# Four residual graph layers on one core: a list schedule with one port for VectorE's two-operand and GpSimd's operations, layer 2's second aggregates placed later, and a buffer of its own for group 1's adjacency

## The chip, the cores and the metric

The kernel runs on one core of a Trainium2 chip. The metric is the device time of one execution in microseconds (us). The kernel before takes 2507.59 us, the median of three runs (2506.04 to 2507.76). Its trace was taken in one profiled execution of 2507.6 us.

## The reference

There are 128 graphs of 128 nodes with 512 features each, and one adjacency of 128x128 per graph. Four layers follow each other. Each adds its result to x and normalises every row of the sum. All is float32.

```python
deg = adj.sum(-1)
d   = (deg + 1) ** -0.5
L   = d[:, :, None] * (adj + I) * d[:, None, :]
# layer 0
x = layernorm(x + relu((L @ x) @ W0 + b0))
# layer 1
q, k = split(x @ Wqk.T, 2);  v = x @ Wv.T          # 64 features each in q and k
w = softmax(((q @ k.T) / 8 * adj).sum(-1), over nodes)
x = layernorm(x + w[:, :, None] * v)
# layer 2
agg = (adj @ x) / max(deg, 1e-6)
x = layernorm(x + relu(concat([x, agg]) @ W2.T))
# layer 3
x = layernorm(x + L @ (x @ W3 + b3))
```

The kernel computes layer 0 and layer 3 as (L @ x) @ W, and layer 3's bias as the row sums of L times b3.

## The kernel before

**Tiles and stages.** The 128 graphs are worked on in 32 groups of G = 4. A group's x is one tile of 128 nodes by 4 graphs by 512 features, and it stays in place through all four layers. The four graphs form two pairs q; in each pair, r = 0 or 1 names the graph. "The first half" below is r = 0, graphs 0 and 2; "the second half" is r = 1, graphs 1 and 3.

A product of a group with a 512x512 weight (`project`, line 511 and below) is taken by blocks of 256 with seven block products in the place of eight, in Winograd's form. Their names are B11, T1, B21, B22, T2, T3 and T4. Four of them need sums of blocks of the left operand (`left_sums`, tiles s1 to s4) and of the weight (`weight_sums`, made once). The left operand has the features on the partitions. It is either an aggregate (`aggregate`, line 452 and below: TensorE multiplies x by a transposed adjacency, and ScalarE copies the result out of the tile p_agg), or a transpose of x, named xT1 for layer 1 and xT2 for layer 2. In the loop x is transposed through DRAM and by VectorE (`turn_x`), at the start and the end by TensorE (`turn_on_tensor`). Layer 2 has two left operands, xT2 and agg2, so each of its products has twice the matmuls.

The results of the products are combined on VectorE in the blocks u5, u2, sa and sb, which are added to x. In the profile they carry an o, for layers 0, 2 and 3, or a v, for layer 1 (u_o, s_v, x<-u_v). A half of x is then normalised by `norm_stats`: VectorE makes the statistics (bnv, mvo), GpSimd the reciprocal root, ScalarE applies them. Layer 3 is normalised by `norm_last`, on ScalarE. PSUM is held in five buffers "pb", for the products (p_o, p_v), and three "pt", for aggregates, transposes and small products. The matmuls are float32, and each shows as two records in the profile. One block product of a group in layers 0, 1 and 3 has 16 records, one of layer 2 has 32; an aggregate of one graph has 8.

`hooks` of a `project` name work that TensorE does right after one of its products; `tails` holds the last product of a `project` until `finish_tails` issues it.

**The order of the work.** `begin` handles groups 0 and 1 through their first layers (lines 814 to 837). After it, each turn t of the loop (lines 840 to 861) interleaves four groups' stages: layer 0 of group t, the load and preparation of group t+1, layer 2 of group t-1, the aggregates of layer 0 of group t+1, layer 1 of group t, layer 3 of group t-1, and at the end the transposes and aggregates of layer 2 of group t. What is left of the last group follows on lines 863 to 870, pair by pair.

**The planner.** Nothing is issued while this code runs. Class `Plan` records every operation with what it reads and writes (`record`, `touch`), and `schedule` (lines 194 to 255) then orders each engine's queue as a list schedule. TensorE's operations keep the order in which the code states them. Every other operation has a due time, worked back from the TensorE operation that needs it (lines 207 to 216). `estimate` (line 284) gives each a duration. The loop at lines 225 to 254 then takes, engine by engine, the operation with the earliest due time among those whose operands are ready. `emit` issues all of them from line 263, so that every row of the profile shows L263; rows are told apart by engine, operation and tile. Each engine works through its own queue in order, so an operation that waits holds everything behind it.

**Preparation of a group.** `load(t)` issues adj and x on SP (the DMA queue's own engine). The tag "adj" has one buffer, so adj of t+1 can only land when VectorE has used that of t. `prep_rows` makes on VectorE deg (row sums of adj), dh, dm, rdeg and the two matrices in `ana`, with the power d on GpSimd. `prep_transpose` turns `ana` on TensorE (tile p_a, into anT and arT) for the first groups, and `prep_turn` does it through DRAM in the loop.

**Layer 1's weights.** `l1_scores` gives, on VectorE, scr, w and rs; TensorE transposes w (p_w); then mx, e and the division make a softmax, and TensorE turns it back (p_ws, ws). All of it stands between layer 1's first products.

Of the kernel before, what the change touches and what calls it, by code (L numbers as in the profile page):

```python
# [18 lines left out]
G = 4  # L19
# [99 lines left out]

class Op:  # L120
    def __init__(self, engine):
        self.engine, self.dur, self.lat, self.size, self.calls, self.preds, self.succs = engine, 0, 0, 0, [], set(), []
        self.last, self.start, self.end = float("inf"), None, None


class Plan:

# [27 lines left out]
    def record(self, engine, method, args, kw):  # L157
        op = self.group if self.group is not None and engine == "tensor" else Op(engine)
        op.calls.append((method, args, kw))
        dur, op.lat, op.size = self.est(engine, method, args, kw)  # L160
        op.dur += dur
        out = kw.get("out", args[0] if args else None)
        outs = [v for v in (out, kw.get("accum_out")) if isinstance(v, Ref)]
        ins = [v for k, v in list(enumerate(args)) + list(kw.items())
               if isinstance(v, Ref) and v is not out and k != "accum_out"]
        for v in ins:
            self.touch(op, v, False)
        for v in outs:
            self.touch(op, v, True)
        op.preds.discard(op)  # L170
        if op is not self.group:
            self.ops.append(op)
# [21 lines left out]
    def schedule(self):  # L194
# [21 lines left out]
            op.last = min(op.last, due - op.dur)  # L216
        queue = {e: [] for e in self.ENGINES}
        waiting = {op: len(op.preds) for op in self.ops}
        free, bus = dict.fromkeys(self.ENGINES, 0), 0
        pe = [op for op in self.ops if op.engine == "tensor"]  # L220
        for op in self.ops:
            if not op.preds:
# [2 lines left out]
        while len(done) < len(self.ops):  # L225
            best = None
            for e in self.ENGINES:
                q = queue[e]
                if e == "tensor":
                    q = [c for c in q if c[2] is pe[0]]  # L230
                if not q:
                    continue
                at = max(free[e], min(c[0] for c in q))
                pick = min((c for c in q if c[0] <= at), key=lambda c: (c[2].last, c[1]))
                for c in q:
                    if at < c[0] < at + pick[2].dur and c[2].last < at + pick[2].dur and c[2].last < pick[2].last:
                        pick, at = c, c[0]
                if best is None or at < best[0]:
                    best = at, e, pick
            at, e, pick = best  # L240
            queue[e].remove(pick)
            op = pick[2]
            op.start, op.end = at, at + op.dur
            free[e] = op.end
            if e == "sync":
                bus = max(bus, op.end + self.LAND) + op.size / self.BUS
                op.lat = max(op.lat, bus - op.end)
            if e == "tensor":
                pe.pop(0)
            done.append(op)  # L250
            for s in op.succs:
                waiting[s] -= 1
                if not waiting[s]:
                    queue[s.engine].append((max(p.end + self.hop(p, s) for p in s.preds), number[s], s))
# [29 lines left out]
def estimate(engine, method, args, kw):  # L284

    out = args[0]
    n = out.idx.size if isinstance(out, Ref) else 0
    if engine == "tensor":
        return (max(109, 0.85 * n) if method == "transpose" else 2 * max(100, 0.833 * n + 2.5)), 100, 0
    if method == "dma_start":  # L290
        size = max(int(np.prod(v.shape)) if isinstance(v, bass.AP) else v.idx.size * 32 * len(v.quads) for v in args)
        return 470, Plan.LAND + size / 60, size
    if engine == "scalar":
        return (380 if method == "activation" else 160) + 0.83 * n, 0, 0
    if engine == "gpsimd":
        if ALU.pow in args:
            return 400 + 150 * n, 0, 0
        return 250 + 2.2 * n, 0, 0
    if method in ("bn_stats", "tensor_reduce"):
        n = args[1].idx.size  # L300
    both = [v for v in args[1:] if isinstance(v, Ref) and v.idx.size == n and v.tile.args[3]["tag"] not in ("pb", "pt")]
    return 160 + (1.3 if len(both) > 1 else 1.04) * n, 0, 0

@with_exitstack
def kernel(
# [30 lines left out]
    st = {}  # L338

    def load(t):  # L340
        a = ap.tile([P, G, P], FP, tag="adj", name=f"adj_{t}", bufs=1)
        nc.sync.dma_start(a, adj[t * G:(t + 1) * G].rearrange("g n m -> n g m"))
        xi = xp.tile([P, G, F], FP, tag="x", name=f"x_{t}")
        for g in range(0, G, 2 if t == 0 else G):
            k = slice(g, g + (2 if t == 0 else G))
            nc.sync.dma_start(xi[:, k], x[t * G:(t + 1) * G][k].rearrange("g n f -> n g f"))
        st["adj", t], st["x", t] = a, xi


    load(0)  # L350

    def weight(src, name, queue, turned=False):

# [153 lines left out]
    def finish_tails():  # L507
        while tails:
            tails.pop(0)()

    def project(name, t, parts, first, c11, fin, hooks=None, after=lambda: None, early=True,
# [7 lines left out]
        def region():  # L519
            return ps_b.tile([P, 2, H], FP, tag="pb", name=f"p_{name}_{t}")[:, qs]  # L520

        def product(p, k, fresh):
            with nc.unit():
                for q in pairs:
                    for i, (left_, w) in enumerate(parts):
                        for c in range(2):
                            nc.tensor.matmul(p[:, q - pairs[0], :], left_[k][:, q, c, :], w[:, k, c, :],
                                             start=(fresh and q == pairs[0] and i == 0 and c == 0),
                                             stop=(i == len(parts) - 1 and c == 1), skip_group_check=True)
            for f in hooks.get(k, ()):  # L530
                f()
# [105 lines left out]
    def l0_out(t, hooks=None, pairs=(0, 1)):  # L637
# [13 lines left out]
            nc.vector.tensor_tensor(c, p, bias(0), ALU.add)  # L651
            fin(0, 0, c)

        project("o0", t, [(st["agg0", t], w0_sb)], first, c11, fin, hooks, pairs=pairs)


    def l1_turn(t, turn=turn_x):
        left("xT1", t)
        for r in range(2):
            turn("xT1", t, r)  # L660
        st["x1T", t] = st["xT1", t]
        left_sums("xT1", t)

    def l1_qk(t, r):

# [59 lines left out]
    def l1_out(t, hooks=None):  # L725
# [14 lines left out]
        def weights():  # L740
            l1_weights(t)
            for f in pending:
# [1 line left out]

        pending = []
        hooks[T3] = [weights] + hooks[T3]
        project("v", t, [(st.pop(("xT1", t)), wv_sb)], copy_first, lambda p, b: fin(0, 0, p), fin, hooks,
                early=False, when=when)


# [3 lines left out]
            turn_x("xT2", t, r)  # L754
        left_sums("xT2", t)

    def l2_agg(t):
        left("agg2", t)
        for g in (0, 2, 1, 3):
            aggregate("agg2", t, g, st["arT", t])  # L760
        left_sums("agg2", t)

    def l2_both(t):

        left("xT2", t)
        left("agg2", t)
        for r in range(2):
            turn_on_tensor("xT2", t, r)
            for g in (r, 2 + r):
                aggregate("agg2", t, g, st["arT", t])  # L770
        left_sums("xT2", t, nc.vector)
        left_sums("agg2", t)

    def l2_out(t, hooks=None, pairs=(0, 1)):
        fin = relu_add(t, pairs)
        project("o2", t, [(st["xT2", t], w2x_sb), (st["agg2", t], w2a_sb)],
                copy_first, lambda p, b: fin(0, 0, p), fin, hooks, pairs=pairs)


# [18 lines left out]
    def l3_out(t, left="agg3", pairs=(0, 1)):  # L798
        def fin(r, h, blk):
            z = half(st["x", t], r, h, pairs)  # L800
            nc.vector.tensor_tensor(z, blk, z, ALU.add)

        project("o3", t, [(st[left, t], w3_sb)], copy_first, lambda p, b: fin(0, 0, p), fin,
                after=lambda: store(t), pairs=pairs)

    def store(t):
# [7 lines left out]
    def begin():  # L814

        prep_rows(0)
        load(1)
        prep_transpose(0)
        weight_sums(w0_sb, nc.gpsimd)
        l0_agg(0, nc.vector, ONE_BY_ONE)  # L820
        prep_rows(1)
        l0_out(0, {B21: [lambda: prep_transpose(1)], B22: [lambda: l0_agg(1)]})
        finish_tails()
        weight_sums(wv_sb, nc.vector)
        l0_out(1)
        l1_turn(0, turn_on_tensor)
        finish_tails()
        for r in range(2):
            l1_qk(0, r)
        for w in (w2x_sb, w2a_sb, w3_sb):  # L830
            weight_sums(w, nc.gpsimd)
        l1_turn(1)
# [1 line left out]
        finish_tails()  # L834
        for r in range(2):
            l1_qk(1, r)
        l2_both(0)

    begin()
    for t in range(1, NT):  # L840
        u = t - 1
        if t > 1:
            l0_out(t)
        if t < last:
            load(t + 1)
            prep_rows(t + 1)
            prep_turn(t + 1)
        if t > 1:
            tails.append(lambda: l1_turn(t))
        l2_out(u, {T3: [lambda: l1_qk(t, 0)]} if t > 1 else {})  # L850
        if t < last:
            l0_agg(t + 1)
        finish_tails()
# [4 lines left out]
        l3_out(u)  # L858
        if t < last:
            l2_turn(t)  # L860
            l2_agg(t)

    l2_both(last)
    for q in range(2):
        l2_out(last, pairs=(q,))
    for q in range(2):
        l3_agg_pair(last, q, nc.gpsimd)
        l3_bias(last, (2 * q, 2 * q + 1))
# [34 lines left out]
```

## Time and profile before

| | before |
|---|---|
| median of three runs | 2507.59 us |
| profiled execution | 2507.6 us |
| its span, first to last instruction | 2505.8 us |
| mean granted TensorE clock | 0.996 |
| TensorE matmul busy | 2466.6 us, 98% |
| VectorE busy | 1785.2 us, 71% |
| GpSimd busy | 1350.2 us, 54% |
| ScalarE busy | 973.2 us, 39% |
| HBM | 96 GB/s over the span |

PE is TensorE, PEld its weight loads, DVE VectorE, ACT ScalarE, POOL GpSimd, SP the engine that issues DMAs. A row such as `2.46 DVE L263 ... x<-s_v,ws,x ... x2` begins with the time from the span's start and the length, both in us, of a run of like instructions on one engine, and gives then the output, the inputs, the shapes and the number of instructions. `[0.19 <-DVE u_o]` says that the engine had been idle for 0.19 us and that VectorE's writing of u_o ended it. A row of a table of windows gives the stretch, its length, and then for TensorE, its weight loads, VectorE, ScalarE and GpSimd the busy time with the number of instructions; the granted clock, DMA's busy share and GB/s close it. A row of waits gives the waiting engine and tile, who ended the wait, the sum in us, the number of waits, and the longest.

### The profile page before, as it was taken

Reading aid. Unit: us, or ns where it says so; the run is one execution under the profiler, and the core shown is the slowest. Engines: PE = TensorE matmul, PEld = TensorE weight load, DVE = VectorE, ACT = ScalarE, POOL = GpSimd, SP = SyncE. Lnnn points to the kernel's source line nnn. Section 1 sums busy time; section 2 is a strip of 40 time slices with the busy share of each in tenths; the row PEclk is TensorE's granted clock in tenths of the full one; section 3 lists DMA queues with packets and bytes.
Section 4 is the critical chain, followed back from the end, with each engine's and each line's share of the span. In section 5 each row is a group of like instructions: output and inputs, shape, how many; then the busy total and the mean of one; then the engine's idle time right before and its main releaser. Section 6 shows DMA issues by size and latency. Waiting matters only on the chain.

```text
span 2505.8 us, 37042 instructions
## 1 busy us (share of the span) xinstructions
PE 2466.6 (98%) x13470; PEld 2204.4 (88%) x13470; DVE 1785.2 (71%) x3161; ACT 973.2 (39%) x1981; POOL 1350.2 (54%) x1530
## 2 busy tenths in 40 slices
PE   8899999999999999999999999999999999999998
PEld 7788888888898888888888888888888888888887
DVE  7677677777767776777777677777777676777665
ACT  2344334343344433343433344333434333343335
POOL 6446455555556464554645555545646455555453
PEclk9999999999999999999999999999999999999999
DMA  5232424333344324243343433343432424433210
GB/s 176 68 97 68 122 80 123 110 78 100 96 106 115 101 72 122 81 123 109 70 108 83 120 110 96 81 109 93 122 109 64 114 81 122 110 95 78 81 55 34
DMA packets 398806, 243.35 MB, mean 97 GB/s; under 512 B 140832, under 2 KB 365600, under 8 KB 398624
## 3 DMA queue, kind: packets, MB, share of 16 engines
q1 hardware_dynamic: 398624, 240.98, 35.9%
q8 instruction: 107, 1.75, 0.3%
q14 instruction: 75, 0.61, 0.1%
HBM read 127.66 MB, written 113.25 MB: 96 GB/s over the span
## 4 chain that ended last, share of the span: by engine, by line
PE 75%; DVE 10%; DMA 5%; POOL 4%; SPq 2%; issue 2%; ACT 2%; DVEq 0%; ACTq 0%; POOLq 0%
PE p_o L263 44%; PE p_v L263 14%; PE p_agg L263 12%; DVE x L263 4%; PE p_qk L263 3%; SPq L263 2%; POOL xT2s L263 2%; ACT x L263 1%; DMA xT1s<-x 1%; DVE u_o L263 1%; DMA xT1y<-xT1s 1%; DMA adj<-in_adj_dram 1%; DVE bnv L263 1%; DVE s_v L263 1%; PE p_sc L263 1%
## 5 line engine op out<-in xcount | busy, mean ns | idle before, releaser
L263 ACT COPY agg<-p_agg 128x512 f32<-128x512 f32 x384 | 225.2, 586 | 730.0 <-PE p_agg L263 730.0
L263 PE MATMUL p_o<-w_sb,agg 128*128 128x256 f32 x1536 | 353.7, 379 | 2.7 <-ACT s_o L263 1.4
L263 PEld LDWEIGHTS p_o<-w_sb,agg 128*128 128x128 f32 x1536 | 286.4, 190 | 40.5 <-ACT s_o L263 2.2
L263 POOL TENSOR_TENSOR xT1s<-xT 128x512 f32<-128x512 f32 x64 | 84.1, 1315 | 381.1 <-DVE xT L263 369.0
L263 PE MATMUL p_o<-w2x_sb,xT2s 128*128 128x256 f32 x1024 | 262.8, 379 | 0.0
L263 PE MATMUL p_o<-w2a_sb,agg2s 128*128 128x256 f32 x1024 | 262.8, 379 | 0.0
L263 POOL TENSOR_TENSOR agg3s<-agg 128x512 f32<-128x512 f32 x62 | 84.1, 1357 | 330.0 <-ACT agg L263 330.0
L263 PE MATMUL p_agg<-anT,x 128*128 128x128 f32 x2048 | 243.9, 277 | 0.3 <-DVE anT L263 0.3
L263 PEld LDWEIGHTS p_agg<-anT,x 128*128 128x128 f32 x2048 | 235.4, 192 | 1.3 <-DVE anT L263 0.6
L263 PE MATMUL p_v<-wv_sb,xT1s 128*128 128x256 f32 x1024 | 233.3, 381 | 0.0
L263 PE MATMUL p_o<-w_sb,agg3s 128*128 128x256 f32 x992 | 226.6, 381 | 5.8 <-DVE u_o L263 5.7
L263 PE MATMUL p_o<-w_sb,agg0s 128*128 128x256 f32 x1024 | 227.7, 380 | 1.0 <-DVE u_o L263 1.0
L263 PEld LDWEIGHTS p_o<-w_sb,agg3s 128*128 128x128 f32 x992 | 185.9, 190 | 41.4 <-POOL rstdv L263 17.4
L263 PEld LDWEIGHTS p_o<-w_sb,agg0s 128*128 128x128 f32 x1024 | 195.2, 191 | 28.0 <-DVE u_o L263 1.4
L263 PEld LDWEIGHTS p_o<-w2x_sb,xT2s 128*128 128x128 f32 x1024 | 194.6, 190 | 26.5
L263 PEld LDWEIGHTS p_o<-w2a_sb,agg2s 128*128 128x128 f32 x1024 | 194.6, 190 | 26.4
L263 PEld LDWEIGHTS p_v<-wv_sb,xT1s 128*128 128x128 f32 x1024 | 189.6, 190 | 26.2
L263 POOL TENSOR_TENSOR agg2s<-agg 128x512 f32<-128x512 f32 x64 | 81.9, 1280 | 236.1 <-ACT agg L263 236.1
L263 DVE STREAM_TRANSPOSE xT<-xT1y 128x512 f32<-128x512 f32 x124 | 80.9, 690 | 168.1 <-DMA xT1y<-xT1s 168.1
L263 PE MATMUL p_o<-w2x_sb,xT 128*128 128x256 f32 x768 | 197.4, 379 | 0.7 <-ACT s_o L263 0.7
L263 ACT ACTIVATE x<-x,nmro,rstdo 128x512 f32<-128x512 f32 x257 | 195.9, 807 | 4.4 <-DVE dm L263 0.2
L263 PE MATMUL p_o<-w2a_sb,agg 128*128 128x256 f32 x768 | 197.1, 379 | 0.0
(138 smaller groups left out, 4760.2 us busy)
## 6 DMA issues: line engine op xcount, KB each, us to landing
x<-in_x_dram SPq DMA_DIRECT2D x31, 1024.0 KB, 6.6
xT1s<-x SPq DMA_DIRECT2D x124, 256.0 KB, 2.7
xT1y<-xT1s SPq DMA_DIRECT2D x248, 128.0 KB, 3.0
out_dram<-x SPq DMA_DIRECT2D x31, 1024.0 KB, 5.6
xT2s<-x SPq DMA_DIRECT2D x120, 256.0 KB, 2.6
xT2y<-xT2s SPq DMA_DIRECT2D x240, 128.0 KB, 3.3
sa<-ana SPq DMA_DIRECT2D x120, 128.0 KB, 3.4
ya<-sa SPq DMA_DIRECT2D x120, 128.0 KB, 3.9
```

The source lines that it names most:

```text
L263: getattr(getattr(self.nc, op.engine), method)(*[v.real() if isinstance(v, Ref) else v for v in args], **{k: v.real() if isinstance(v, Ref ...
```

## The change

The number of instructions on every engine stays as it is. The order in which the engines do them changes, and one buffer.

1. *A port in the plan.* `Op` has a flag `port`. `estimate` sets it for every GpSimd operation and for a VectorE operation on two full operands of which neither is in PSUM. In `schedule` an operation with the flag cannot be placed before the previous one with the flag has ended, on whichever of the two engines. The durations in the plan change: GpSimd 250 + 2n ns (2.2n before), VectorE on two such operands 1.12n (1.3n), the shortest matmul 104 ns (100).
2. *Group 1's adjacency.* `load(1)` comes right after `load(0)`, ahead of all weights. Its adj tile lies in one of the three buffers "y" and no longer waits for the one buffer "adj".
3. *Layer 2's second aggregates.* `l2_agg(t, r)` makes one half. The first half stays at the end of a turn; the second half moves into the next turn, to just after the B21 of layer 0 of the next group. The sums agg2s follow it. `operand` looks a left operand up when its product is stated, since the sums may not exist yet when `project` is called.
4. *Start and end.* `l2_both` is split in the same way, with aggregates ahead of transposes and all of its sums on VectorE. In `begin`, group 1's transposes of `ana` move from behind B21 to behind B11 of group 0's layer 0, that layer's tail is no longer finished at once, and layer 1's transposes and q, k products of group 0 are done half by half. The preparation of group 2 is stated in the hook of group 0's layer 2.

```diff
     def record(self, engine, method, args, kw):
...
-        dur, op.lat, op.size = self.est(engine, method, args, kw)
+        dur, op.lat, op.size, op.port = self.est(engine, method, args, kw)
...
     def schedule(self):
...
-        free, bus = dict.fromkeys(self.ENGINES, 0), 0
+        free, bus, port = dict.fromkeys(self.ENGINES, 0), 0, 0
...
+                q = [(max(c[0], port if c[2].port else 0),) + c[1:] for c in q]
                 at = max(free[e], min(c[0] for c in q))
...
+            if op.port:
+                port = op.end
...
     if engine == "gpsimd":
-        if ALU.pow in args:
-            return 400 + 150 * n, 0, 0
-        return 250 + 2.2 * n, 0, 0
+        return (400 + 150 * n if ALU.pow in args else 250 + 2 * n), 0, 0, True
...
-    return 160 + (1.3 if len(both) > 1 else 1.04) * n, 0, 0
+    return 160 + (1.12 if len(both) > 1 else 1.04) * n, 0, 0, len(both) > 1 and n > 32
...
     def load(t):
-        a = ap.tile([P, G, P], FP, tag="adj", name=f"adj_{t}", bufs=1)
+        if t == 1:
+            a = tp.tile([P, 2, G, P], FP, tag="y", name="adj_1", bufs=3)[:, 0]
+        else:
+            a = ap.tile([P, G, P], FP, tag="adj", name=f"adj_{t}", bufs=1)
...
     load(0)
+    load(1)
...
-    def l2_agg(t):
-        left("agg2", t)
-        for g in (0, 2, 1, 3):
+    def l2_agg(t, r):
+        if r == 0:
+            left("agg2", t)
+        for g in (r, 2 + r):
             aggregate("agg2", t, g, st["arT", t])
-        left_sums("agg2", t)
+        if r == 1:
+            left_sums("agg2", t)
+
+    def l2_both(t, r):
+
+        if r == 0:
+            left("xT2", t)
+            left("agg2", t)
+        for g in (r, 2 + r):
+            aggregate("agg2", t, g, st["arT", t])
+        turn_on_tensor("xT2", t, r)
+        if r == 1:
+            left_sums("xT2", t, nc.vector)
+            left_sums("agg2", t, nc.vector)
...
-        l0_out(0, {B21: [lambda: prep_transpose(1)], B22: [lambda: l0_agg(1)]})
-        finish_tails()
+        l0_out(0, {B11: [lambda: prep_transpose(1)], B22: [lambda: l0_agg(1)]})
         weight_sums(wv_sb, nc.vector)
         l0_out(1)
-        l1_turn(0, turn_on_tensor)
+        l1_turn(0, turn_on_tensor, (0,))
         finish_tails()
-        for r in range(2):
-            l1_qk(0, r)
+        l1_qk(0, 0)
+        l1_turn(0, turn_on_tensor, (1,))
+        l1_qk(0, 1)
...
-        l2_both(0)
+        l2_both(0, 0)
...
         if t > 1:
-            l0_out(t)
+            l0_out(t, {B21: [lambda: l2_agg(u, 1)]})
+            prep(t + 1)
...
-        l2_out(u, {T3: [lambda: l1_qk(t, 0)]} if t > 1 else {})
+        l2_out(u, {T3: [lambda: l1_qk(t, 0)]} if t > 1 else {B21: [lambda: l2_both(0, 1), lambda: prep(2)]})
...
         if t < last:
             l2_turn(t)
-            l2_agg(t)
+            l2_agg(t, 0)
-
-    l2_both(last)
+    l2_both(last, 0)
     for q in range(2):
-        l2_out(last, pairs=(q,))
+        l2_out(last, {B21: [lambda: l2_both(last, 1)]} if q == 0 else {}, (q,))
```

## The prediction

> **What bounds the kernel now.** I read, in this order, the page's busy shares, the windows of 80 us, TensorE's own waits, the chain that ended last, and the timeline where these point.
>
> ```profile
> span 2505.8 us, 37042 instructions
> PE 2466.6 (98%) x13470; PEld 2204.4 (88%) x13470; DVE 1785.2 (71%) x3161; ACT 973.2 (39%) x1981; POOL 1350.2 (54%) x1530
> ```
>
> TensorE is the bound. The profiled execution took 2507.6 us, 1.8 more than its span, and the median of the runs shown is 2507.59, so what the sum takes from the span it takes from the median.
>
> ```profile
> 0.00:80.00 80.00, 65.60 (x365) 56.96 (x366) 58.21 (x99) 22.00 (x42) 51.10 (x53) 0.96 0.56 165
> 80.00:160.00 80.00, 73.21 (x399) 65.33 (x399) 51.56 (x92) 28.43 (x58) 34.08 (x36) 0.96 0.27 60
> 160.00:240.00 80.00, 79.81 (x436) 71.44 (x435) 58.36 (x103) 32.65 (x70) 44.89 (x51) 1.00 0.37 96
> ```
>
> The first number behind the length is TensorE's busy time: full from 160 us on, and short by 14.4 + 6.8 us before. Only idle TensorE can be won back, so I list it.
>
> ```profile
> PE p_o L263 <- DVE u_o L263: 7.6, 33, 1.0
> PE p_a L263 <- DVE ana L263: 6.1, 2, 5.5
> PE p_xT L263 <- ACT xT2y L263: 6.0, 2, 5.5
> PE p_w L263 <- DVE rs L263: 3.2, 7, 1.0
> ```
>
> Two long waits, at 16 and 84 us, are the start's; 33 short ones and seven at p_w belong to the loop. Ends of matmuls are modelled, so I price a wait by starts. In the chain, the stretch of 24 p_v matmuls (5.18 us) comes once an iteration, at 512.72, 589.60, 666.57 and 743.12 us: steps are 76.55 us as a rule (the last of these) and longer in seven iterations (here 76.88 and 76.97; the longest 77.68). The excesses 0.32 + 0.42 + 0.33 + 0.71 + 0.90 + 1.13 + 0.57 make **4.4 us**. They end at p_w:
>
> ```profile
> 1356.27 0.69 DVE L263 TENSOR_REDUCE deg<-adj 128x4 f32<-128x512 f32 x1 [3.73 <-DMA adj<-in_adj_dram]
> ...
> 1358.35 0.27 PE L263 MATMUL p_w<-ident,w 128*4 128x128 f32 x1 [0.97 <-DVE rs L263]
> ```
>
> VectorE stands at deg, for the next group's adjacency, and layer 1's scr, w and rs, which TensorE wants, are queued behind it. Inside every iteration there is the layer 3 wait:
>
> ```profile
> 1371.94 2.46 DVE L263 SCALAR_TENSOR_TENSOR x<-s_v,ws,x 128x256 f32<-128x256 f32 x2
> ...
> 1372.74 3.62 PE L263 MATMUL p_o<-w_sb,agg3s 128*128 128x256 f32 x16
> ...
> 1374.33 1.27 DVE L263 BATCH_NORM_STATS2 bnv<-x 128x6 f32<-128x512 f32 x2
> ...
> 1375.73 0.67 DVE L263 TENSOR_TENSOR u_o<-p_o,s_o 128x512 f32<-128x512 f32 x1
> ...
> 1376.55 3.69 PE L263 MATMUL p_o<-w_sb,agg3s 128*128 128x256 f32 x16 [0.19 <-DVE u_o L263]
> ```
>
> Sixteen matmuls at 0.216 us (160 take 34.54) from 1372.74 end their turn at 1376.20; the next begins at 1376.55, and its sixteen take 3.69 for 3.62. So 0.35 + 0.08 = 0.43 us, 31 times: **13.2 us**.
>
> **The change, part by part.** Instruction counts stay the same; only order, waits and a buffer change.
>
> *Layer 3 and layer 1 in the loop (the new costs and the port in the plan).* In the changed program u_o of layer 3 stands ahead of the two bnv. The product that it reads ends near 1374.5, so u_o runs to about 1375.4 instead of 1376.4, 0.8 us before TensorE needs it at 1376.20: −13.2 us. deg moves behind scr, w, rs and the first u_v, ahead of mx; in the worst iteration deg, dh and dm are through 1.0 us after 1356.27, and mx cannot run before p_w, then at 1357.2, has ended: −4.4 us. If the adjacency came 1 us later still, mx would be late, but e needs to be there only for p_ws, 5.3 us after p_w. Behind u_o, the normalisation of layer 1's second half becomes some 2 us later.
>
> [...] The row: x<-s_v takes 1.23 us each beside GpSimd's sums, where the same form x<-u_v has a mean of 0.487. [...] By the plan, which now keeps them apart, 2 × 0.74 = 1.5 us of VectorE would be saved here each iteration; [...] no wait is added, and these two stand where they stood. I take the rows, no saving; either way the sum is the same, since VectorE (71%) does not set the end.
>
> *Second aggregates later in the loop.* Eight matmul records per graph, two graphs, 16 × 0.111 = 1.78 us, move behind layer 0's B11, layer 3's T4 and layer 0's B21 (3 × 1.73 us): no time of TensorE, and 5.2 us of cover for the later normalisation. The POOL sums agg2s start 5 us later, near 1389.3 for 1384.5; seven sums of 1.3 to 1.7 end at 1400, and the first two that TensorE needs are at 1395.5 for its T1 at 1404. Price 0; without that slack it would be 1.3 us per sum late. On SP one half of xT2's second store now stands before the first half's loads (+0.3 us), and layer 0's second store before the first's loads of xT1: these start near 1408.6 for 1405.4, land 3 to 5 us later, and two transposes of 0.65 put xT at 1414.7 to 1416.7; TensorE wants it at 1417.8. Price 0, with 1 to 3 us to spare. The out store moves behind them and delays the next x by 5 us; that x is used an iteration later.
>
> *The start.* Group 1's adjacency is the third load instead of the eleventh or so (12.02 us, when VectorE had freed the buffer). It puts the w0 loads back by 0.5 us. Walking the changed order with durations of before: d_1 stands behind POOL's first w0 sum, which waits for w0 (10.65, now near 11.2), so d_1 ends near 13.9; ana times d, beside a POOL sum, took 1.74: 15.6. TensorE waits there 1.75 us, not 5.55. The six agg0s on VectorE go one per POOL sum (11.20, 12.24, 13.65, 14.94 before) and hold T2 and B22 back by 1.0 + 1.15; group 1's aggregates begin at 25.6 for 31.02. Half of this is lost again: POOL's agg0s of group 1 now stands behind one sum each of w2a and w2x, whose last loads SP issues near 34.0 and which land near 36.3; T1 starts at 39.2 for 43.56, after 3.2 us of idleness, and deg_2, which waits for adjacency 2 near 37.4, puts u_o at 45.0. Layer 1's first product starts at 56.3 for 60.61. Then the xT1 transposes stand behind bnv (+0.5 us), but layer 2's first half needs only its own normalisation: its B11 starts at 56.3 + 24.0, B21 at + 28.3, the second half's aggregates and turns at + 31.75, and T1, after copies and sums, at + 36.9 = 93.2. Before: 102.81. **−9.6 us.** From both sides: nothing, if w2x lands 5 us later, and −14, if POOL never waits for it.
>
> ```profile
> 82.03 2.05 PE L263 MATMUL p_agg<-arT,x 128*128 128x128 f32 x16
> ...
> 89.62 1.97 PE L263 MATMUL p_xT<-ident,xT2y 128*128 128x128 f32 x8 [5.54 <-ACT xT2y L263]
> 91.38 3.62 PE L263 MATMUL p_agg<-arT,x 128*128 128x128 f32 x16
> ```
>
> This shows why the long waits cost more than their length: behind 5.54 us of idleness the same 16 matmuls took 3.62 instead of 2.05, some 2.5 us in all; behind 1.2 us (77.15) they did not slow. My 3.2 us lies between. [...] by the row of 5.54, 2.5 us more. I take none and keep 2.5 for the range.
>
> *The end.* The last group's second half comes in the B21 of its first pair, with its sums for all four graphs: aggregates and turns end at 10.9 us behind layer 3's T3, four copies (12.1) and two sums (0.69 each) let T1 start at 13.0. Before it was 2459.63 − 2448.78 = 10.85. **+2.1 us**; between 0, if the copies overtake ScalarE's row sums, and 3.
>
> **Sum:** 2507.6 − 13.2 − 4.4 − 9.6 + 2.1 = **2482.5 us**.
>
> **Rivals.** *The start gives nothing* (w2x late, a slow stretch): 2507.6 − 17.6 + 2.1 = 2492.1. For it: POOL and VectorE both stand behind loads at 36 us; against it: two 5.5 us waits go in any case. *The layer 3 wait moves*, to layer 0's u_o or to qk: 2507.6 − 4.4 − 9.6 + 2.1 = 2495.7. For it: only 0.8 us of slack; against: nothing else was added ahead of u_o. *Slower:* the transposes of xT2's first half now stand ahead of layer 0's sums and u_o. If their load comes late, VectorE stands and TensorE's B22 with it. u_o would be ready near 1391.0 for 1391.9; the gains, 25.1 us, are gone at 25.1/31 = 0.8 us a turn, so with a load 1.7 us later than before. At 2.1 us: 2507.6 − 25.1 + 31 × 1.2 = 2519.7. Against it: those transposes came 26.3 to 28.0 us behind p_w, never later. *No effect*, if the orders differ only where nobody waits: 2507.6. *More*: −14 at the start and TensorE without any wait in the tail, 2476.
>
> **How the numbers follow.** 60% for the sum, whose own range is 2476 to 2489; 17% for 2492, 15% for 2496, 3% each for slower and for more, 2% for no effect. 0.2% (5 us) is about what a measurement here tells from no change: faster 0.95, the same 0.02, slower 0.03. The range, 2474 to 2497, leaves out the slow and the unchanged case and little else.
>
> **What would show it.** Steps of p_v of 76.1 us in every iteration; no wait of p_o for u_o in layer 3, and u_o ahead of bnv; deg behind rs, and p_w without waits; near 160 us the loop some 10 us ahead; no half clock at 22 and 89 us, perhaps one at 39; T1 of the last group 13 us behind T3. A step that stays near 76.5, or an idle TensorE for layer 0's B22 or for qk, would prove me wrong, and so would a start with a new wait over 4 us.

## The result, and the profile after

The changed kernel takes 2488.57 us, the median of six runs (2486.55 to 2489.90), against 2506.82 us before in the same session: 18.3 us less, a ratio of 0.9926 with a 95% interval from 0.9913 to 0.9939. I had forecast 2482.5 us, with a range from 2474 to 2497. The sign and the range held; the time lies 6.1 us above the forecast. The page of the changed kernel, in the same two lines as before:

```profile
span 2486.8 us, 37083 instructions
PE 2457.3 (99%) x13470; PEld 2206.9 (89%) x13470; DVE 1810.0 (73%) x3169; ACT 973.2 (39%) x1981; POOL 1334.0 (54%) x1522
```

The span is 19.0 us shorter. VectorE is busy 25 us longer, which costs nothing. Eight of GpSimd's sums have gone over to VectorE (3161 and 1530 instructions before, 3169 and 1522 now), by part 4 of the change; so the counts of these two did not stay, as I had said of all engines. The windows, with TensorE's busy time first behind the length, the granted clock third from the end:

```profile
0.00:80.00 80.00, 64.73 (x348) 56.33 (x349) 54.73 (x98) 22.64 (x43) 48.29 (x53) 0.94 0.55 165
80.00:160.00 80.00, 77.53 (x438) 69.56 (x437) 54.91 (x102) 31.02 (x65) 31.58 (x34) 0.99 0.27 60
160.00:240.00 80.00, 80.00 (x438) 71.90 (x437) 59.86 (x103) 30.34 (x63) 44.63 (x51) 1.00 0.36 96
...
320.00:2400.00 2080.00, 2080.00 (x11417) 1871.32 (x11416) 1529.84 (x2659) 816.21 (x1659) 1136.53 (x1286) 1.00 0.38 100
2400.00:2490.00 90.00, 75.03 (x401) 65.86 (x399) 50.93 (x107) 42.45 (x93) 27.35 (x51) 0.96 0.07 24
```

From 160 to 2400 us TensorE is never idle. Idleness is left in the start, 15.3 us in the first window where it was 14.4 and 2.5 in the second where it was 6.8, and at the very end. TensorE's own waits say the same; the columns are the sum, the number and the longest:

```profile
PE p_o L266 <- DVE u_o L266: 6.4, 3, 4.5
PE p_qk L266 <- DVE xT L266: 3.9, 1, 3.9
PE p_o L266 <- DVE xT2s L266: 3.1, 2, 1.6
PE p_a L266 <- DVE ana L266: 1.6, 1, 1.6
...
PE p_o L266 <- POOL agg30s L266: 1.3, 1, 1.3
```

Of the 33 waits for u_o three are left, none of them in the loop, and p_w is gone from the list. New are q and k of group 1 (3.9 us) and one u_o of 4.5 us; both lie in the start. In the loop VectorE now stands like this:

```profile
1340.14 0.42 DVE L266 TENSOR_TENSOR scr<-p_sc,qs 128x256 f32<-128x256 f32 x1 [0.79 <-PE p_sc L266]
...
1342.97 0.68 DVE L266 TENSOR_REDUCE deg<-adj 128x4 f32<-128x512 f32 x1
...
1359.77 0.69 DVE L266 TENSOR_TENSOR u_o<-p_o,s_o 128x512 f32<-128x512 f32 x1 [0.34 <-PE p_o L266]
1360.38 0.68 DVE L266 BATCH_NORM_STATS2 bnv<-x 128x6 f32<-128x512 f32 x1
```

deg comes behind scr and no longer waits for its adjacency; u_o of layer 3 waits for TensorE, not the reverse, and stands ahead of bnv. By the starts of p_w, group by group, the 19.0 us divide so:

| stretch | before | after | difference | forecast |
|---|---|---|---|---|
| start, to p_w of group 2 | 206.24 | 201.48 | -4.8 | -9.6 |
| 28 turns, p_w of group 2 to 30 | 2147.89 | 2131.55 | -16.3 | -17.6 for the whole loop |
| the last turn, to p_w of group 31 | 72.93 | 72.51 | -0.4 | |
| end, p_w of group 31 to the last matmul | 70.24 | 72.76 | +2.5 | +2.1 |

Layer 3 of one group lies in the first row and that of another in the last, and each was 0.4 us longer before. Counted with the loop, as the forecast has it, they make the loop's gain 17.6 us, the start's 4.4 and the end's loss 2.9. All 28 steps are 76.13 us.

### The profile page after: what moved, and what is told of

The parts are those of the page before. It is cut to its first block, busy times and chain, and to the rows that moved or that the text cites. A ratio compares the mean times of both kernels' runs of the same rounds, so it can differ in the third digit from the quotient of the medians.

```text
span 2486.8 us, 37083 instructions
## 1 busy us (share of the span) xinstructions
PE 2457.3 (99%) x13470; PEld 2206.9 (89%) x13470; DVE 1810.0 (73%) x3169; ACT 973.2 (39%) x1981; POOL 1334.0 (54%) x1522
## 3 DMA queue, kind: packets, MB, share of 16 engines
q8 instruction: 107, 1.75, 0.3%
## 4 chain that ended last, share of the span: by engine, by line
PE 97%; SPq 1%; DVE 1%; DMA 1%; ACT 0%; issue 0%; POOL 0%; ACTq 0%; POOLq 0%; DVEq 0%
PE p_o L266 61%; PE p_v L266 16%; PE p_agg L266 14%; PE p_qk L266 5%; PE p_sc L266 1%; SPq L266 1%; DMA x<-in_x_dram 0%; DVE x L266 0%; PE p_ws L266 0%; ACT xT L266 0%; PE p_w L266 0%; DMA adj<-in_adj_dram 0%; PE p_xT L266 0%; ACT agg L266 0%; DVE wv_sb L266 0%
## 5 line engine op out<-in xcount | busy, mean ns | idle before, releaser
L266 POOL TENSOR_TENSOR xT1s<-xT 128x512 f32<-128x512 f32 x64 | 94.1, 1471 | 290.2 <-DVE xT L266 220.1
L266 PE MATMUL p_o<-w_sb,agg3s 128*128 128x256 f32 x992 | 219.2, 379 | 0.0
L266 PEld LDWEIGHTS p_o<-w2a_sb,agg2s 128*128 128x128 f32 x1024 | 194.6, 190 | 26.5
L266 DVE TENSOR_TENSOR u_o<-p_o,s_o 128x512 f32<-128x512 f32 (+1 forms) x132 | 89.2, 675 | 145.3 <-PE p_o L266 145.3
L266 PE MATMUL p_v<-wv_sb,xT 128*128 128x256 f32 x768 | 181.6, 379 | 0.9 <-DVE u_v L266 0.9
```

The lines of the kernel that those rows point to most:

```text
L266: getattr(getattr(self.nc, op.engine), method)(*[v.real() if isinstance(v, Ref) else v for v in args], **{k: v.real() if isinstance(v, Ref ...
```

## The experiments

For each run the span (one profiled execution) and the median of its timed runs are given. The expectations are as written before each run. "Put back" or "placed" means the order of VectorE's or GpSimd's own queue; nothing else is changed where the text doesn't say so.

### The loop: which part makes the gain

**Port alone.** Part 1 of the change on the kernel before.

```diff
-        return (max(109, 0.85 * n) if method == "transpose" else 2 * max(100, 0.833 * n + 2.5)), 100, 0
+        return (max(109, 0.85 * n) if method == "transpose" else 2 * max(104, 0.833 * n + (2.5 if n > P else 5))), 100, 0, False
...
+                q = [(max(c[0], port if c[2].port else 0),) + c[1:] for c in q]
...
+            if op.port:
+                port = op.end
```

> The kernel before with the port and the new durations alone; adjacency 1, layer 2's aggregates, start and end stay as before. In its plan u_o of layer 3 already stands ahead of bnv, but deg still stands ahead of scr. Theory A (the port alone makes the loop's gain, by moving u_o): steps of 76.13 us, no wait of p_o for u_o in layer 3, 13.2 us less by this, of the 4.4 us at p_w only some 1 to 2 back, since dh and dm alone have moved; with a start and an end like those of before 2492 to 2496 us. Theory B (it is the second aggregates' later place that lets u_o go first): steps of 76.55 us, and 2503 to 2508.

Measured: 2495.95 us (span 2493.6), ratio 0.9957 (0.9943 to 0.9972). Steps of 76.19 us, some longer (up to 77.05); 1.3 us of waits at p_w. Theory A holds. The run has the port and the new durations together; no run has the new durations alone, so the share of each is not shown.

**No port.** The changed kernel with the old `estimate` and `schedule`.

```diff
-                q = [(max(c[0], port if c[2].port else 0),) + c[1:] for c in q]
...
-    return 160 + (1.12 if len(both) > 1 else 1.04) * n, 0, 0, len(both) > 1 and n > 32
+    return 160 + (1.3 if len(both) > 1 else 1.04) * n, 0, 0
```

> The changed kernel without the port and with the durations of before in its plan; all else as changed. Here bnv stands ahead of u_o again, and deg ahead of scr. Theory A: steps of 76.55 us with some longer ones, so 13.2 + about 4.4 us more in the loop than the changed kernel; its start has another order too, which I hold to be within 5 us: 2501 to 2511. Theory B (the aggregates' later place is what pays): steps of 76.13 and 2485 to 2492.

Measured: 2531.11 us (span 2529.7), ratio 1.0109 (1.0083 to 1.0135): slower than before by 25 us, far beyond both expectations. Its waits:

```profile
PE p_w L263 <- DVE rs L263: 26.5, 23, 3.2
PE p_o L263 <- DVE u_o L263: 9.6, 33, 2.7
```

The layer 3 wait is back, as theory A says. But the wait at p_w is not the 3.2 us of before, it is 26.5. The 28 steps take 2175.57 us, 27.7 more than before. Something in the rest of the change lengthens that wait, and the plan with the port hides it. The start is not what is lost: p_w of group 2 comes at 200.52 us, where it came at 206.24 before and at 203.26 with the port alone.

**Second aggregates later, alone.** One edit on the kernel before.

```diff
-            l0_out(t)
+            l0_out(t, {B21: [lambda: l2_agg(u, 1)]})
...
-            l2_agg(t)
+            l2_agg(t, 0)
```

> The kernel before with one edit: in the loop layer 2's second aggregates stand behind B21 of the next layer 0. No port, durations, start and end of before. Theory (without the port this edit is what costs no_port its 27.7 us in the loop: it shifts VectorE's ana, and with it the next adjacency, by some 2 us, while deg stays ahead of scr): steps of 76.6 to 80 us, waits of p_w of about 26 us in all, 2530 to 2540 us. Rival (the loss came from no_port's other edits): steps of 76.55, 2503 to 2510.

Measured: 2535.03 us (span 2531.4), ratio 1.0113 (1.0096 to 1.0130), steps of 76.55 to 78.97. So this edit costs 27 us when nothing else is changed. deg stands ahead of scr in this kernel too, and the next adjacency comes later. Its load is issued 5.8 us ahead of p_w (mean of 26 turns), and p_w itself is late by 1.1 us a turn, so the load stands 4.7 us ahead of p_w's due start. Before, these are 6.0, 0.2 and 5.9: the load is issued 1.2 us later. One turn, VectorE and then TensorE:

```profile
1280.10 1.75 DVE L263 TENSOR_TENSOR ana<-adj,rdeg 128x512 f32<-128x512 f32 x1
...
1288.25 0.69 DVE L263 TENSOR_REDUCE deg<-adj 128x4 f32<-128x512 f32 x1 [3.19 <-DMA adj<-in_adj_dram]
```

```profile
1290.34 0.27 PE L263 MATMUL p_w<-ident,w 128*4 128x128 f32 x1 [1.17 <-DVE rs L263]
```

**Second aggregates back.** The changed kernel with these aggregates at the end of the turn.

```diff
-            l0_out(t, {B21: [lambda: l2_agg(u, 1)]})
+            l0_out(t)
...
             l2_agg(t, 0)
+            l2_agg(t, 1)
```

> The changed kernel with layer 2's second aggregates back at the end of a turn in the loop; port, start and end as changed. Its plan has u_o ahead of bnv, and deg ahead of scr again, dh and dm behind rs. Theory (the later place pays only together with the port, by letting deg fall behind rs): steps of 76.19 and some up to 77, as in the run of the port alone: 5 us longer than the changed kernel, 2492.5 to 2495. Rival (the place of these aggregates is worth nothing of its own): 2488 to 2489.5.

Measured: 2493.34 us (span 2492.7), steps of 76.19 and up to 77.26, 2.2 us of waits at p_w. The edit is worth 4.8 us together with the port and costs 27 without it.

**u_o behind bnv again.** `hoists` is a list of pairs; `emit` issues the first of each just ahead of the second.

```diff
+        for op, before in self.hoists:
...
+        if name == "o3" and t < last:
+            a, b, c, d = mark["v", t + 1, 1]
+            for op in (a, c, b, d):
+                nc.hoists.append((op, mark[name, t, "u5"]))
```

> The changed kernel with one thing put back by hand in the loop: the two bnv and mvv of layer 1's second half stand ahead of layer 3's u_o again on VectorE; every other queue is the same. By my sum 0.43 us a turn in 30 turns: +13 us, to 2501 or 2502. Rival (x<-s_v and all behind it are late anyway, so that the order of u_o and bnv is not what sets the wait): no more than 3 us.

Measured: 2500.96 us (span 2497.3). Its waits for u_o are 12.0 us in 33 places, and every one of the 28 steps is 76.55 or 76.56 us: the 0.43 us come back to the hundredth. (In this execution the start was 2.2 us shorter, so the span shows less than the steps.)

**deg first again.**

```diff
+    for t in range(2, last - 2):
+        for k in ("deg", "dh", "dm"):
+            nc.hoists.append((mark[k, t + 3], mark["scr", t]))
```

> The changed kernel with deg, dh and dm of the group three ahead put back ahead of scr of layer 1 in 27 turns; every other queue is the same. By my sum the irregular waits at p_w come back, 4.4 us in all (2 to 7, by when each adjacency lands): 2490.5 to 2495.5. Rival (the waits came from SP's queue, whose order the change also moved, and not from VectorE's): no waits at p_w, and within 1 us of the changed kernel.

Measured: 2493.02 us (span 2491.5). p_w waits 3.0 us in three places by the list; the steps, small excesses included, sum to 2135.73, 4.2 more than the changed kernel's. Expected were 4.4.

This run says more. Its second aggregates stand late and deg stands ahead of scr, as in the run that lost 27 us, and it loses 4.2. So the place of deg alone is not what hides the 27. The adjacency comes earlier here: its load is issued 6.4 us ahead of p_w's due start (mean of 26 turns), for 4.7 there. The load waits until VectorE has used the last adjacency, and the last to use it is the third `ana`. In the second aggregates' own run and then in this one, from 320 to 2320 us (number, busy us, mean ns, idle us before):

```profile
L263 DVE TENSOR_TENSOR ana<-adj,rdeg 128x512 f32<-128x512 f32 x26 | 45.5, 1752 | 0.0
L275 DVE TENSOR_TENSOR ana<-adj,rdeg 128x512 f32<-128x512 f32 x26 | 17.6, 678 | 0.0
```

It takes 0.69 us before, 1.75 with the later aggregates alone, and 0.68 again where port and later aggregates come together. These 1.1 us are nearly the whole 1.2 by which the later aggregates alone put the load back, and 1.1 of the 1.7 by which it comes earlier here. The rest is an earlier place in the queue. That place can count for as much: the port alone has 1.75 us too, but starts the third ana sooner, and its load stands as it did before. No run moves the third ana by itself, so this is read from the traces and not shown by an experiment.

**One price in place of the port.** The changed kernel without the port, with its durations and one more:

```diff
-            if op.port:
-                port = op.end
...
+    if method == "scalar_tensor_tensor" and args[1].tile.args[3]["tag"] == "s" and n == 256:
+        return 1230, 0, 0, False
```

> The changed kernel without the port in its plan, with the new durations, and with one price put by hand: x<-s_v of 256 columns 1.23 us, what it takes in the trace. Its plan has u_o ahead of bnv; deg, dh, dm and rdeg stand ahead of scr. Theory (what the port does for u_o is to tell the plan how long two x<-s_v take; it is no matter of keeping engines apart): no wait of p_o for u_o in layer 3, 13 us less than the run without the port, with its waits at p_w: 2510 to 2522. Rival (only the port's own spacing moves the wait): steps of 76.55 and more, 2528 to 2534.

Measured: 2567.47 us (span 2568.4), ratio 1.0237 (1.0220 to 1.0254). Both expectations missed. Its waits, and then ScalarE in one of its turns:

```profile
PE p_sc L264 <- ACT kd L264: 53.7, 28, 3.7
PE p_o L264 <- DVE u_o L264: 4.9, 3, 3.3
```

```profile
827.48 0.20 ACT L264 ACTIVATE nmro<-mro 128x2 f32<-128x2 f32 x1 [6.16 <-POOL mro L264]
827.71 1.52 ACT L264 ACTIVATE x<-x,nmro,rstdo 128x512 f32<-128x512 f32 x2
829.14 0.35 ACT L264 COPY kd<-p_qk 128x256 f32<-128x256 f32 x1
```

The waits for u_o are three again, so one right price is enough for that. But a normalisation of x now stands ahead of kd on ScalarE, ScalarE stands 6.16 us for mro, from GpSimd, and TensorE waits for kd in 28 turns. That the plan without the port believes mro to come earlier than it does is my reading of this; the plan's own times are not shown. The loss has only moved to another engine.

### The start

**deg of group 2 behind u_o.**

```diff
-        nc.vector.tensor_reduce(deg, a, AX.X, ALU.add)
+        op = nc.vector.tensor_reduce(deg, a, AX.X, ALU.add)
+        if t == 2:
+            op.preds.add(mark["o0", 1, "u5"])
```

> The changed kernel with deg, dh of group 2 placed behind u_o of group 1's layer 0 on VectorE; the other queues are the same. In the changed kernel VectorE stands 4.29 us at that deg, for adjacency 2, with two x<-u_o, s_o and sums of wv behind it, and TensorE then waits 4.53 us for u_o and works at half clock behind it, 6.32 us for 3.6. Theory: the wait falls to about 0.7 us (GpSimd's sb_o is ready at 40.5), the half clock goes, layer 1's first product starts near 53 us for 59.25, and the whole is 6 us shorter, 2482 to 2484. Rival (the loads of the weights and GpSimd's sums set the start, so the time is waited for one step later): at most 2 us, 2486.5 to 2489.

In the changed kernel, TensorE:

```profile
37.09 3.74 PE L266 MATMUL p_o<-w_sb,agg0s 128*128 128x256 f32 x16 [1.01 <-POOL agg0s L266]
45.37 6.32 PE L266 MATMUL p_o<-w_sb,agg0s 128*128 128x256 f32 x16 [4.53 <-DVE u_o L266]
...
77.66 5.44 PE L266 MATMUL p_qk<-wqk_sb,xT 128*128 128x128 f32 x32 [3.88 <-DVE xT L266]
```

and VectorE, which makes both late:

```profile
35.92 0.69 DVE L266 TENSOR_REDUCE deg<-adj 128x4 f32<-128x512 f32 x1 [4.29 <-DMA adj<-in_adj_dram]
...
44.55 0.68 DVE L266 TENSOR_TENSOR u_o<-p_o,sb_o 128x512 f32<-128x512 f32 x1
...
72.03 2.96 DVE L266 SCALAR_TENSOR_TENSOR x<-u_v,ws,x 128x256 f32<-128x256 f32 x2
...
76.80 2.49 DVE L266 STREAM_TRANSPOSE xT<-xT1y 128x512 f32<-128x512 f32 x4
```

With deg later, T1, T2 and B22 of group 1 run in one stretch, 7.52 us for 32 matmuls:

```profile
37.20 7.52 PE L267 MATMUL p_o<-w_sb,agg0s 128*128 128x256 f32 x32 [1.41 <-POOL agg0s L267]
```

Measured: 2484.11 us (span 2480.9), 4.5 us less than the changed kernel by the medians and 5.9 by the spans. Layer 1's first product starts at 53.49 us for 59.25. The theory holds, though the time is 0.1 us beyond its range; the wait of q and k stays at 3.9, as it moves along.

**TensorE kept busy.** `keep_busy` is 38 transposes of ident that nobody reads; the plan counts no time for them.

```diff
-        l0_out(1)
+        l0_out(1, {T1: [keep_busy]})
```

> The changed kernel with 38 transposes of the identity put behind T1 of group 1's layer 0, where TensorE stands idle for 4.5 us; they take 38 x 0.109 = 4.1 us and nobody reads them. Theory (idleness is what brings the half clock): the 16 matmuls of T2 and B22 take 3.6 us again for 6.32, and all is 2.7 us shorter, near 2486. Rival (the clock falls there for another reason): they take 6.3, and the time stays at 2488.6.

Measured: 2485.55 us (2484.61 to 2488.84; span 2483.0). The granted clock, in windows of 2 us of the changed kernel (third number from the end), and the matmuls of this run:

```profile
40.00:42.00 2.00, 0.84 (x4) 0.38 (x3) 2.00 (x3) 0.00 (x0) 2.00 (x2) 1.00 1.07 360
42.00:44.00 2.00, 0.00 (x0) 0.00 (x0) 1.93 (x4) 0.00 (x0) 1.99 (x3) 0.97 0.93 343
44.00:46.00 2.00, 0.63 (x2) 0.57 (x3) 2.00 (x6) 0.88 (x2) 0.91 (x2) 0.50 0.60 229
46.00:48.00 2.00, 2.00 (x6) 1.61 (x5) 1.21 (x3) 1.98 (x5) 1.71 (x4) 0.50 0.04 9
48.00:50.00 2.00, 2.00 (x6) 1.58 (x5) 0.69 (x1) 0.00 (x0) 2.00 (x3) 0.50 0.00 0
```

```profile
38.16 4.31 PE L266 MATMUL p_busy<-ident 128*128 128x128 f32 x38
42.31 1.89 PE L266 MATMUL p_o<-w_sb,agg0s 128*128 128x256 f32 x8
44.63 3.69 PE L266 MATMUL p_o<-w_sb,agg0s 128*128 128x256 f32 x16 [0.42 <-DVE u_o L266]
```

In the changed kernel TensorE falls idle at about 40.8 us, the clock halves just ahead of 44, and it stays at 0.50 to beyond 50 (0.83 in the next window). With the gap filled it is 1.00 in every window from 36 to 50 us, and the sixteen take 3.69 us for 6.32. So idleness brought it here, and the price was 2.6 us.

**Sums of w3 later.**

```diff
-        for w in (w2x_sb, w2a_sb, w3_sb):
+        for w in (w2x_sb, w2a_sb):
             weight_sums(w, nc.gpsimd)
         l1_turn(1)
+        weight_sums(w3_sb, nc.gpsimd, mark["xT1", 1, "turn"])
```

> The changed kernel with the four sums of w3 on GpSimd placed behind the transposes of xT1 of group 1. Three of them run now at 70.68 to 74.7 us, beside two x<-u_v of VectorE that take 1.48 us each where the loop's mean is 0.48, and behind these, xT of group 1 is 3.9 us late for q and k. Theory (GpSimd and a two-operand VectorE instruction hold each other up): these x<-u_v take about 0.5 us, xT comes 2 us earlier, and q, k wait 1.9 us and do not slow behind it: 2 to 3.7 us shorter, 2485 to 2486.5. Rival (the load of xT1y, which lands near 74.5, holds it): x<-u_v still speeds up, but q and k wait as before; 2488.6.

Measured: 2484.76 us (span 2483.2), 3.6 us less in the span. VectorE and TensorE:

```profile
70.80 0.48 DVE L267 SCALAR_TENSOR_TENSOR x<-u_v,ws,x 128x256 f32<-128x256 f32 x1
```

```profile
74.72 3.81 PE L267 MATMUL p_qk<-wqk_sb,xT 128*128 128x128 f32 x32 [1.79 <-DVE xT L267]
```

x<-u_v takes 0.48 us where two took 2.96 in all, the wait is 1.79 for 3.88, and the 32 matmuls take 3.81 for 5.44. The theory holds in each number.

**Adjacency 1 in the common buffer.**

```diff
-        if t == 1:
-            a = tp.tile([P, 2, G, P], FP, tag="y", name="adj_1", bufs=3)[:, 0]
...
     load(0)
-    load(1)
...
         prep_rows(0)
+        load(1)
```

> The changed kernel with group 1's adjacency in the one buffer of the others again, and its load stated where it was before; all else as changed. By my walk of the start the early adjacency brings group 1's aggregates 5.4 us forward, of which most is lost at u_o of its layer 0, which waits for adjacency 2 in any case: 1 to 3 us longer, 2489.5 to 2491.5. Rival (the early adjacency carries the whole gain of the start): about 5 us longer, 2493 to 2494, with layer 1's first product 5 us later.

Measured: 2488.94 us (span 2486.8), the same as the changed kernel. p_a waits 9.45 us for 1.56, group 1's aggregates begin at 34.36 for 25.43, and layer 1's first product at 59.47 for 59.25. By then adjacency 2 has come, u_o doesn't wait, and no clock is lost there; it is lost earlier, in and behind the hole of 9.45 us (0.50 in the windows from 20 to 28 us). Both expectations were too high: the buffer of its own is worth nothing in this order. Which of the other changes of the start makes its gain is left open.

**Four moves at once.** deg of group 2 as above, the sums of w2x and w2a behind group 1's agg0s, and those of w3 stated behind group 0's agg2s.

```diff
+            op.preds.add(mark["o0", 1, "u5"])
...
+            weight_sums(w, nc.gpsimd, mark["agg0", 1])
...
-        l2_out(u, {T3: [lambda: l1_qk(t, 0)]} if t > 1 else {B21: [lambda: l2_both(0, 1), lambda: prep(2)]})
+        l2_out(u, {T3: [lambda: l1_qk(t, 0)]} if t > 1 else {B21: [lambda: l2_both(0, 1), lambda: weight_sums(w3_sb, nc.gpsimd, mark["agg2", 0]), lambda: prep(2)]})
```

> The changed kernel with four groups moved at the start, for a shorter time: deg of group 2 behind u_o of group 1 (-5.9 us of span alone), the sums of w2x and w2a on GpSimd behind group 1's agg0s (TensorE's wait of 1.0 to 1.6 us for agg0s goes), and those of w3 behind agg2s of group 0 (-3.6 us by itself, placed behind xT1; here further back). If these add up, 2488.6 - 5.9 - 3.7 - 1.4 = 2477.6, with the loop at 76.13 as it is. Rival (each only uncovers the next wait): no shorter than the best of them alone, 2484.

Measured: 2481.30 us (2480.70 to 2481.94; span 2479.9), ratio to before 0.9898 (0.9883 to 0.9912), steps of 76.13. It is 7.3 us faster than the changed kernel, the fastest of all that were run, and 3.7 slower than the sum. Where the rest went, on VectorE and on GpSimd:

```profile
86.36 0.68 DVE L267 TENSOR_TENSOR agg2s<-agg 128x512 f32<-128x512 f32 x1
86.96 1.75 DVE L267 TENSOR_TENSOR xT2s<-xT 128x512 f32<-128x512 f32 x1
88.74 1.64 DVE L267 TENSOR_TENSOR xT2s<-xT2s,xT 128x512 f32<-128x512 f32 x1
90.30 1.75 DVE L267 TENSOR_TENSOR agg2s<-agg2s,agg 128x512 f32<-128x512 f32 x1
```

```profile
86.61 6.56 POOL L267 TENSOR_TENSOR w_sb<-w_sb 128x512 f32<-128x512 f32 x4
```

The plan has the sums of w3 behind those of agg2. On the chip nothing makes GpSimd wait for that: VectorE stood for deg of the next group until 84.67, and the two sets ran side by side. VectorE's sums took up to 1.75 for 0.68 and GpSimd's 1.64 for 1.27 each, and TensorE waited 3.65 us for layer 2's T1. The clock was 0.50 behind that, and T1's first three groups of four records took 2.04, 1.91 and 1.91 us, where the later ones take 1.03.

## Why the prediction was right or wrong

**Layer 3 in the loop: right.** The step "u_o ahead of bnv, 0.43 us a turn" is shown by the run that puts bnv back. It is the port with its durations that moves it (port alone), and what the port tells the plan counts only as a duration: a price of 1.23 us for x<-s_v moves u_o as well.

**The wait at p_w: right in size, wrong in its cover.** The 4.4 us came, and 4.2 went when deg was put back. But I costed the second aggregates' later place at nothing and named the normalisation's slack as cover. The runs show another price: 27 us without the port, through VectorE's later adjacency. Two things hide it. The larger, by the traces, is that with the port the third ana is done sooner and the load of the next adjacency is issued 1.7 us earlier; the smaller is deg behind rs, the 4.2 us. Neither was in my account. Port and later aggregates are one edit in effect: 44 us of loop lie between the plan with both and the plan without the port. That this edit alone would make the kernel slower was not among my rivals, and that it cost nothing here was luck as far as my reasons go. My slower case, xT2's transposes, did not occur.

**The start: the step that failed.** I forecast 9.6 us and got 4.4 without the layer 3 wait. Up to u_o the walk was close: T1 at 37.1 us (39.2 forecast), u_o read at 45.4 (45.0). Two terms were mis-sized. First, "my 3.2 us lies between. I take none": T1 came earlier and u_o did not. My walk has 3.2 us of idleness ahead of T1 and some 2 ahead of u_o; the chip had 1.01 and 4.53, and the half clock behind them cost 2.6. I had kept 2.5 for the range. Second, I carried over the distances of before behind layer 1's first product (B11 24.0 us later). They hid a new wait: q and k of group 1 wait 3.9 us and lose 1.7 more to the clock, where before they waited 0.5 and 1.1. The w3 run shows half of that wait to be GpSimd's sums beside x<-u_v. Together layer 2's T1 came at 98.3 us, 5.1 later than I had it.

Holes of 4.5 and 3.9 us were both followed by a clock of 0.50. In the first it fell 3.1 us after TensorE stopped, in the second 4.2 us after (idle from 73.8, a clock of 1.00 in the window to 78 and of 0.50 from there), when work had begun again. By the shares of the windows it was back at 50.7 us, 5.3 behind the start of work, and at 81.4, 3.7 behind it. So it was at half for 6.8 and for 3.4 us. The price of a hole differed from one execution to the next as well. In the run with u_o behind bnv, whose queues are the same up to there, the first hole was just as long, and the clock was at half for 3.4 us only:

```profile
44.37 5.27 PE L275 MATMUL p_o<-w_sb,agg0s 128*128 128x256 f32 x16 [4.53 <-DVE u_o L275]
```

The sixteen took 5.27 us for 6.32, and p_w of group 2 came at 199.26 us for 201.48. A single execution of the start is known no better than that. Nor did the length of a hole alone decide. In the run of one price the clock was 0.50 behind a hole of 1.97 us, in the window from 832 to 834 us, and eight matmuls took 2.90 us for 1.95:

```profile
829.64 1.11 PE L264 MATMUL p_sc<-kd,arT 128*128 128x65 f32 x8 [1.97 <-ACT kd L264]
830.58 2.90 PE L264 MATMUL p_v<-wv_sb,xT1s 128*128 128x256 f32 x8
```

In the run with w3 later, a hole of 2.57 us (92.26 to 94.83) left the clock at 1.00. To take none at 3.2 us was my estimate between two rows, one of 1.2 us without a loss and one of 5.54 with it, and it was not a safe one.

**The end: T1 right, one wait not seen.** Measured 2.9 for 2.1. I had T1 at 13.0 us behind layer 3's T3, by the copies and sums of the second half's new place. It came 12.7 behind it (2426.83 to 2439.57) for 10.9 before, and waited 1.58 us for xT2s. The kernel without the port has the same, so the new place alone is enough for it (2470.73 to 2483.47, 12.7):

```profile
2470.73 1.95 PE L263 MATMUL p_agg<-arT,x 128*128 128x128 f32 x16
...
2483.47 1.13 PE L263 MATMUL p_o<-w2x_sb,xT2s 128*128 128x256 f32 x4 [1.57 <-DVE xT2s L263]
```

But with the port the old order would have been no better. The port alone has T1 12.5 us behind T3 (2434.05 to 2446.53), by another wait:

```profile
2437.97 0.65 PE L266 MATMUL p_xT<-ident,xT2y 128*128 128x128 f32 x4 [1.10 <-ACT xT2y L266]
```

TensorE waits there for a transpose's input that the kernel before had in time. That this is the late normalisation behind u_o, which I had called covered, is the likely reason and not shown. The other 0.9 us come from GpSimd's agg30s, which TensorE waits 1.30 us for in both kernels with the port and not in the one without it. I had not seen it.

**VectorE and GpSimd.** At the start of the changed kernel two x<-u_v took 1.48 us each beside GpSimd's sums, and 0.48 each in the w3 run, where these were moved. My estimate that the two x<-s_v would stand where they stood held, at 1.265 us before and after. Others moved. In the loop x<-u_o fell from 1.24 to 0.89 us, while ana with the identity rose from 1.30 to 1.70 and anT times d from 0.69 to 1.73; VectorE was busy 27 us longer in the 28 turns. So VectorE's time did not fall, but where its long instructions lay counted, as at the third ana (1.75 us with the later aggregates alone, 0.68 with the port as well).

## What to carry to other kernels

A list schedule is as good as what it knows. Told to keep two kinds of operation apart, this one did not make VectorE's time shorter (27 us longer in 28 turns), and still paid: operations behind a long one were put in a better order (u_o ahead of bnv, 0.43 us a turn), and an instruction on which a load depended became short (the third ana). Price an edit together with the instruction that waits first in an engine's queue (deg here, 3.19 us in the turn shown, with scr behind it), and with what lets its load start: the same move of two aggregates cost 27 us under one plan and brought 5 under another. And where a start is walked step by step, don't carry over distances of the old trace past a point where anything was moved: each holds waits that may grow.

## What the hardware showed that I had not expected

A hole of 4.5 us cost TensorE 2.6 us more behind it in one execution and 1.6 in another, and with 38 useless transposes in it the kernel was 3.0 us faster by the medians and 3.8 by the spans (the slowest of those runs lies among the changed kernel's). Behind a hole of 2.0 us the clock was 0.50 (the run of one price), and behind one of 2.6 us it stayed at 1.00 (w3 later). In the run of four moves two sets of sums ran side by side on VectorE and GpSimd and took up to 1.75 and 1.64 us each, for 0.68 and 1.27 elsewhere: VectorE lost 1.07 us, more than the whole length of its own instruction, GpSimd 0.37, somewhat under a third.
